# Five elementwise steps of a scan moved from VectorE to GpSimd and ScalarE

## The chip, the cores and the metric

The kernel runs on one core of a Trainium2 chip. A core has five engines that take their instructions in order, each from a queue of its own: TensorE (PE in the profile, its weight loads PEld), VectorE (DVE), ScalarE (ACT), GpSimd (POOL) and SyncE (SP), which only issues DMAs here. They wait for each other by semaphores. Data lies in SBUF and, for the outputs of matmuls, in eight banks of PSUM. The metric is the time of one execution on the device, in microseconds; less is better.

## The reference, cut to what matters

Input are 16 sequences of 512 tokens with 128 channels, float32. A block adds four parts to them, one after the other: an attention with rotated features, a mixture of experts, a selective scan, and the same mixture of experts again; each works on the layer norm of what is there. The change touches the scan, for which the reference is:

```python
xz = jnp.einsum('btd,ed->bte', x, W_in)
xp, z = (xz[..., :D_INNER], xz[..., D_INNER:])          # D_INNER = 256
xc = conv(xp, conv_w) + conv_b                          # causal, 4 taps, by channel
xc = _silu(xc)
ssm = jnp.einsum('bti,si->bts', xc, W_x)
Bp, Cp = (ssm[..., :D_STATE], ssm[..., D_STATE:])       # D_STATE = 16
dt = jax.nn.softplus(jnp.einsum('bti,oi->bto', xc, W_dt) + b_dt)
A = -jnp.exp(A_log)
def step(h, inp):
    x_t, b_t, c_t, dt_t = inp
    dA = jnp.exp(dt_t[..., None] * A)
    h = dA * h + dt_t[..., None] * b_t[:, None, :] * x_t[..., None]
    y_t = jnp.einsum('bds,bs->bd', h, c_t)
    return (h, y_t)
_, ys = lax.scan(step, h0, (tm(xc), tm(Bp), tm(Cp), tm(dt)))
y = (y - mu) * lax.rsqrt(var + LN_EPS) * ln_g + ln_b    # mu, var over the 256 channels
y = y + xc * D_param
y = y * _silu(z)
return jnp.einsum('bti,di->btd', y, W_out)
```

## The kernel before

A sequence is the unit of work: 512 tokens along the free dimension, 128 channels on the partitions (two halves for the 256 channels of the scan). Sequences are taken in pairs. For each of the eight pairs there are four parts: `attention` for both, `ffn` over both together, `scan` for both, `ffn` again with the output.

**The order is made by a planner.** No engine operation is issued where the code describes it. `pe`, `dve`, `act`, `pool` and `g_.add(SP, ...)` put a step into a list, with its engine, an estimated time in microseconds, and the buffers that it reads and writes. `Program.emit` then walks through this list with one clock per engine. Of the steps whose inputs are there and whose buffers are free it takes, for each engine, one that can start within 0.25 us, and among those the one with the smallest `prio`; a step that needs another table of ACT counts as late by 1 us. The engine order that comes of this is fixed in the program, and the real engines follow it whatever the real durations are. `prio` is set in the last lines of `hybrid_block`: the parts of a pair get spans of it (`SPANS`), within which it grows in proportion to the sum of the estimated times. Pair b's scans span b + 1.5 to b + 2.5, the attention of the next pair b + 1 to b + 2, so the two run beside each other. Where the planner sees PE idle for over 0.5 us after little work, it puts in matmuls with zeros (`add_zeros`, L379). A table of ACT is loaded in `emit` (L191) when a step names another one than the last.

**The scan** of one sequence goes through these steps; the lines are those of the profile:

- A layer norm and a transpose (`normed`, L411 to L444). L932 clears the left edge of the tile `pad`.
- For each half c: a projection (L938), its copy to `pad` (ACT, L939), the convolution's first product with its bias (DVE, L942) and three more taps (DVE, L951).
- For each half: a second projection and SiLU for z (L961, L962), SiLU for xc (ACT, L963).
- The matmuls for B and C with their copies (L984, L987), and for the step sizes dt (L996), of which ACT makes |v| (L999) and max(v, 0) (L1000).
- Softplus with a corrected logarithm, for each half o: exp(-|v|) (ACT, L1004), + 1 (DVE, L1005), the logarithm (ACT, L1006), the rounding error of the sum 1 + e (DVE, L1009), the logarithm less this error (DVE, L1013), and added to max(v, 0) (DVE, L1014).
- dt times xc for both halves in one POOL instruction (L1016), and xc times D on ACT (L1020).
- The main part, 32 units of 128 rows (8 channels by 16 states) in 17 steps: PE spreads dt x and dt over the rows (L1050), DVE multiplies by B (L1056), ACT takes exp (L1061), DVE scans along the tokens (L1064), POOL multiplies by C (L1068), PE sums over the states (L1078), and ACT copies y out (L1084).
- The layer norm over the channels: PE's mean (L1096), DVE subtracts it (L1102), ACT squares (L1104), PE's mean of the squares (L1096), and 1/std by `rsqrt`: ACT's logarithm and exponential (L394, L395), then on DVE a Newton step with a square (L397) and three more operations (L398 to L400).
- For each half: y times 1/std (DVE, L1110), times the gain plus xc (DVE, L1113), times z (POOL, L1119). Then the projection (PE, L1126), added to x (DVE, L1129).

`rsqrt` has two callers: here, with a tile of 128x512, and `normed`, with a tile of 128x4.

The tiles `xc`, `z`, `dt`, `sp_u`, `s1`, `Bw` and `Cw` exist once, so one scan follows another. Temporary tiles of 128x512 come from 28 buffers (`half`), with a number for each kind.

**Beside the scan** runs the attention of a later pair. For each pair of units: PE's two products (L541), ACT's logarithm and exponential for a reciprocal (L548, L549), DVE's two operations (L550, with PSUM; L557, with PSUM), POOL's product (L561) and PE's sum (L569). The mixture of experts has a DVE addition (L884) and a GELU (ACT, L887) for each block of rows, the weights by DMA of SP, and a scatter and a gather of rows by DMAs that POOL issues (L797, L909); DVE adds the gathered rows (L921).

Of the kernel before, what the change touches and what calls it, by code (L numbers as in the profile page):

```python
# [12 lines left out]
AF = mybir.ActivationFunctionType  # L13
ALU = mybir.AluOpType
AX = mybir.AxisListType

P = 128
D = 128
N = 512
# [201 lines left out]
def hybrid_block(ctx: ExitStack, tc: tile.TileContext, io: dict, out: bass.AP):  # L221
    nc = tc.nc
# [10 lines left out]
    def sb(tag, shape, bufs=1, dtype=F32):  # L233
        if tag not in places:
            places[tag] = Slots(work, tag, shape, bufs, dtype)
        return Buf(places[tag], tag)
# [22 lines left out]
    def load(name, shape, src=None, eng=None):  # L259
        t = const.tile(list(shape), F32, name=name)  # L260
        (eng or nc.sync).dma_start(out=t, in_=io[name] if src is None else src)
        return t
# [30 lines left out]
    cw = load("cw", [P, NH, KC])  # L293
# [53 lines left out]
    conv_b, b_dt, d_par, ln_g, ln_b = (cols[:, i, :] for i in range(5))  # L347
# [12 lines left out]
    def tmp(kind):  # L360
        return Buf(half, kind)
# [4 lines left out]
    def psum(kind="mm"):  # L366
        return Buf(bank, kind)
# [7 lines left out]
    def pe(us, fn, r, w, claim=(), work=None):  # L375
        g_.add(PE, us, fn, r, w, claim=claim, work=work)
# [6 lines left out]
    def dve(us, fn, r, w):  # L383
        g_.add(DVE, us, fn, r, w)

    def pool(us, fn, r, w):
        g_.add(POOL, us, fn, r, w)

    def act(us, fn, r, w, table=None):
        g_.add(ACT, us, fn, r, w, table)  # L390

    def rsqrt(rs, v, c, shape, tag, us):

        act(us[0], lambda: nc.scalar.activation(rs(), c(v()), AF.Ln, bias=eps), [v], [rs], LNEXP)  # L394
        act(us[0], lambda: nc.scalar.activation(rs(), rs(), AF.Exp, scale=-0.5), [rs], [rs], LNEXP)  # L395
        q = tmp(tag) if shape == [P, N] else sb(tag, shape, 2)
        dve(us[1], lambda: nc.vector.tensor_tensor(q(), rs(), rs(), ALU.mult), [rs], [q])  # L397
        dve(us[1], lambda: nc.vector.scalar_tensor_tensor(q(), c(v()), eps, q(), ALU.add, ALU.mult), [v, q], [q])  # L398
        dve(us[1], lambda: nc.vector.tensor_scalar(q(), q(), -0.5, 1.5, ALU.mult, ALU.add), [q], [q])
        dve(us[1], lambda: nc.vector.tensor_tensor(rs(), rs(), q(), ALU.mult), [rs, q], [rs])  # L400

    def normed(xts, who, bufs):
# [3 lines left out]
        for k, xt in enumerate(xts):  # L406
# [11 lines left out]
            dve(0.6, aggr, [st], [mv])  # L418
            rs = sb("rs", [P, NT], 3)
            rsqrt(rs, mv, lambda t: t[:, :, 1], [P, NT], "q", (0.25, 0.16))  # L420
            mr = sb("mr", [P, NT], 3)
            dve(
# [504 lines left out]
    def scan(b, xs):  # L927
        xt = xs[b]
        _, xnT = normed([xt], "", 2)
        pad, xc, z = sb("s1", [P, NH, KC - 1 + N]), sb("xc", [P, NH, N]), sb("z", [P, NH, N])  # L930
# [5 lines left out]
        for c in range(NH):  # L936
            pz, cv = psum(), tmp("cv")
            pe(MM, lambda c=c, pz=pz: mm(pz(), win[:, c * P : (c + 1) * P], xnT(), start=True, stop=True), [xnT], [pz], [pad, cv, xc, z])  # L938
            act(0.59, lambda c=c, pz=pz: nc.scalar.copy(pad()[:, c, KC - 1 :], pz()), [pz], [(pad, c)])  # L939
            dve(  # L940
                0.55,
                lambda c=c, cv=cv: nc.vector.tensor_scalar(  # L942
                    cv(), pad()[:, c, 0:N], cw[:, c, 0:1], conv_b[:, c : c + 1], ALU.mult, ALU.add
                ),
                [(pad, c), (pad, "edge")],
                [cv],
            )
            for k in range(1, KC):
                dve(
                    0.72,  # L950
                    lambda c=c, k=k, cv=cv: nc.vector.scalar_tensor_tensor(  # L951
                        cv(), pad()[:, c, k : k + N], cw[:, c, k : k + 1], cv(), ALU.mult, ALU.add
                    ),
                    [(pad, c), (pad, "edge"), cv],
                    [cv],
                )
            cvs.append(cv)
            yield
# [31 lines left out]
        dt, ex, up = sb("dt", [P, NH, N]), sb("s1", [P, NH, KC - 1 + N]), sb("sp_u", [P, NH, N])  # L990
# [10 lines left out]
        for o in range(NH):  # L1001
            ln = tmp("sg")
            e_, u_, d_ = (lambda o=o: ex()[:, o, 0:N]), (lambda o=o: up()[:, o, :]), (lambda o=o: dt()[:, o, :])
            act(0.63, lambda e_=e_: nc.scalar.activation(e_(), e_(), AF.Exp, scale=-1.0), [(ex, o)], [(ex, o)], LNEXP)  # L1004
            dve(0.37, lambda e_=e_, u_=u_: nc.vector.tensor_scalar_add(u_(), e_(), 1.0), [(ex, o)], [(up, o)])  # L1005
            act(0.63, lambda u_=u_, ln=ln: nc.scalar.activation(ln(), u_(), AF.Ln), [(up, o)], [ln], LNEXP)  # L1006
            dve(
                0.74,
                lambda e_=e_, u_=u_: nc.vector.scalar_tensor_tensor(u_(), u_(), -1.0, e_(), ALU.add, ALU.subtract),  # L1009
                [(up, o), (ex, o)],  # L1010
                [(up, o)],
            )
            dve(0.7, lambda u_=u_, ln=ln: nc.vector.tensor_tensor(ln(), ln(), u_(), ALU.subtract), [ln, (up, o)], [ln])  # L1013
            dve(0.7, lambda d_=d_, ln=ln: nc.vector.tensor_tensor(d_(), d_(), ln(), ALU.add), [(dt, o), ln], [(dt, o)])  # L1014
        dtx = sb("s1", [P, NH, KC - 1 + N])
        pool(2.35, lambda: nc.gpsimd.tensor_tensor(dtx()[:, :, 0:N], dt(), xc(), ALU.mult), [dt, xc], [dtx])  # L1016

# [5 lines left out]
        y = sb("sp_u", [P, NH, N])  # L1023
# [8 lines left out]
        for n in range(len(two) + 1):  # L1032
            work_ = []
            if n < len(two):
                c, j, q0 = two[n]
# [4 lines left out]
            if n:  # L1040
                c, j, q0 = two[n - 1]
# [15 lines left out]
            if n:  # L1057
                c, j, q0 = two[n - 1]
# [46 lines left out]
        rs = tmp("sg")  # L1105
        var = over_channels(sq, [rs])
        rsqrt(rs, var, lambda t: t, [P, N], "cv", (0.65, 0.68))
        yield
        for c in range(NH):
            dve(0.7, lambda c=c: nc.vector.tensor_tensor(y()[:, c, :], y()[:, c, :], rs(), ALU.mult), [(y, c), rs], [(y, c)])  # L1110
            dve(
                0.74,
                lambda c=c: nc.vector.scalar_tensor_tensor(  # L1113
                    y()[:, c, :], y()[:, c, :], ln_g[:, c : c + 1], xc()[:, c, :], ALU.mult, ALU.add
                ),
                [(y, c), (xc, c)],
                [(y, c)],
            )
            pool(1.27, lambda c=c: nc.gpsimd.tensor_tensor(y()[:, c, :], y()[:, c, :], z()[:, c, :], ALU.mult), [(y, c), (z, c)], [(y, c)])  # L1119
# [19 lines left out]
    def scans(bs):  # L1139
        for b in bs:  # L1140
            yield from scan(b, xs)
# [91 lines left out]
```

## Time and profile before

| | |
|---|---|
| Median of 3 runs | 4292.2 us (4279.41 to 4292.76) |
| Profiled execution | 4297.67 us |
| Its span, first to last instruction | 4295.8 us |
| Instructions | 62640 |
| Mean granted clock of PE | 0.929 |
| DMA | 296.99 MB, mean 69 GB/s |
| Table loads of ACT (L191) | 327 of 1283 ns, 419.5 us |

The profiled execution is one run of its own; sums that are made from the profile are made against its time, and it lies 5.5 us above the median. In a row of the groups of instructions stand the line, the engine, the operation, output and inputs by the program's names, the shapes, the number of instructions, then the busy time in us and the mean of one in ns, and last the idle time of the engine just before them, with what ended most of it. Tiles of `half` are called half, banks of PSUM bank, `pad`, `ex`, `dtx` and the squares s (they share `s1`), and `up` and `y` sp_u.

### The profile page before, as it was taken

Reading aid. Unit: us, or ns where it says so; the run is one execution under the profiler, and the core shown is the slowest. Engines: PE = TensorE matmul, PEld = TensorE weight load, DVE = VectorE, ACT = ScalarE, POOL = GpSimd, SP = SyncE. Lnnn points to the kernel's source line nnn. Section 1 sums busy time; section 2 is a strip of 40 time slices with the busy share of each in tenths; the row PEclk is TensorE's granted clock in tenths of the full one; section 3 lists DMA queues with packets and bytes.
Section 4 is the critical chain, followed back from the end, with each engine's and each line's share of the span. In section 5 each row is a group of like instructions: output and inputs, shape, how many; then the busy total and the mean of one; then the engine's idle time right before and its main releaser. Section 6 shows DMA issues by size and latency. Waiting matters only on the chain. (4 is left out here: it accounts for less than half of the span.)

```text
span 4295.8 us, 62640 instructions
## 1 busy us (share of the span) xinstructions
PE 3967.1 (92%) x20444; PEld 2038.1 (47%) x20444; DVE 3380.3 (79%) x5863; ACT 2850.6 (66%) x4661; POOL 2614.1 (61%) x2202
## 2 busy tenths in 40 slices
PE   7999999989999999999999999999999999987975
PEld 2345344445354454534545345454545445553554
DVE  7975878877888778888797887979788887756772
ACT  6777667567676577766768667686767667544541
POOL 6765855756666466675575765756766656544351
PEclk9999999989999799998999899998999989898996
DMA  2004003104131131310414013131223214141443
GB/s 66 1 27 127 9 26 87 48 28 120 33 95 56 28 114 54 104 36 28 125 45 124 12 47 109 56 115 32 71 72 93 67 30 121 44 126 38 115 127 107
DMA packets 397770, 296.99 MB, mean 69 GB/s; under 512 B 29290, under 2 KB 340596, under 8 KB 397444
## 3 DMA queue, kind: packets, MB, share of 16 engines
q1 hardware_dynamic: 380324, 258.87, 21.0%
q0 software_dynamic: 16544, 33.66, 2.7%
q8 instruction: 163, 2.67, 0.3%
q14 instruction: 163, 1.34, 0.1%
q10 hardware_dynamic: 576, 0.46, 0.0%
HBM read 244.32 MB, written 48.56 MB: 68 GB/s over the span
## 5 line engine op out<-in xcount | busy, mean ns | idle before, releaser
L561 POOL TENSOR_TENSOR half<-half,half 128x512 f32<-128x512 f32 x1024 | 1293.6, 1284 | 556.8 <-DVE half L557 438.9
L1068 POOL TENSOR_TENSOR half<-half,Cw 128x512 f32<-128x512 f32 x512 | 641.9, 1272 | 544.8 <-DVE half L1064 464.5
L550 DVE TENSOR_TENSOR half<-bank,half 128x512 f32<-128x512 f32 x1024 | 689.3, 683 | 190.3 <-ACT half L549 172.7
L541 PE MATMUL bank<-rot,krot 32*128 32x512 f32 x2048 | 770.5, 672 | 29.3 <-DVE half L550 15.9
L557 DVE SCALAR_TENSOR_TENSOR half<-half,bank 128x512 f32<-128x512 f32 x1024 | 667.3, 679 | 162.2 <-PE bank L541 151.5
L548 ACT ACTIVATE half<-bank 128x512 f32<-128x512 f32 x1024 | 598.8, 585 | 281.9 <-PE bank L541 275.1
L549 ACT ACTIVATE half<-half 128x512 f32<-128x512 f32 x1024 | 645.1, 630 | 30.9
L1064 DVE TENSOR_TENSOR_SCAN half<-bank,half 128x512 f32<-128x512 f32 x512 | 599.5, 1207 | 74.8 <-ACT bank L1061 73.3
L541 PE MATMUL bank<-raw,kraw 32*128 32x512 f32 x2048 | 616.3, 664 | 10.7 <-DVE half L550 5.9
L1061 ACT ACTIVATE bank<-bank,A 128x512 f32<-128x512 f32 x512 | 319.2, 658 | 254.7 <-PE bank L1050 249.6
L379 PE MATMUL bank<-cos,zero 128*128 128x512 f32 x850 | 479.0, 672 | 0.0
L879 PE MATMUL bank<-half,w 128*128 128x128 f32 x3000 | 401.1, 283 | 47.1 <-DMA w<-in_W 32.7
L879 PEld LDWEIGHTS bank<-half,w 128*128 128x128 f32 x3000 | 362.8, 194 | 157.8 <-DVE half L884 44.3
L191 ACT ACT_TABLE_LOAD x327 | 419.5, 1283 | 5.7
L1056 DVE TENSOR_TENSOR half<-bank,Bw 128x512 f32<-128x512 f32 x512 | 328.8, 682 | 104.7 <-PE bank L1050 104.3
L891 PEld LDWEIGHTS bank<-w,half 128*128 128x128 f32 x3000 | 353.2, 193 | 100.6 <-ACT half L887 68.5
L891 PE MATMUL bank<-w,half 128*128 128x128 f32 x3000 | 379.3, 281 | 18.9 <-ACT half L887 18.2
L1050 PE MATMUL bank<-dt,over 32*128 32x512 f32 x1024 | 373.6, 672 | 16.7 <-DVE half L550 16.6
L569 PE MATMUL bank<-half,v_sp 128*32 128x512 f32 x2048 | 356.7, 625 | 14.5 <-POOL half L561 13.9
L541 PEld LDWEIGHTS bank<-raw,kraw 32*128 32x128 f32 x2048 | 176.3, 192 | 337.4 <-DVE half L550 69.5
L541 PEld LDWEIGHTS bank<-rot,krot 32*128 32x128 f32 x2048 | 242.4, 192 | 164.7 <-DVE half L550 60.1
L1050 PE MATMUL bank<-s,over 32*128 32x512 f32 x1024 | 307.2, 667 | 8.3 <-POOL s L1016 4.5
(248 smaller groups left out, 5387.1 us busy)
## 6 DMA issues: line engine op xcount, KB each, us to landing
w<-in_W SPq DMA_DIRECT2D x750, 256.0 KB
half<-inr SPq DMA_DIRECT2D x43, 256.0 KB
outr<-half SPq DMA_DIRECT2D x43, 256.0 KB
half<-ins SPq DMA_DIRECT2D x38, 256.0 KB
outs<-half SPq DMA_DIRECT2D x38, 256.0 KB
x<-in_x SPq DMA_DIRECT2D x16, 256.0 KB
out<-x SPq DMA_DIRECT2D x16, 256.0 KB
inr<-xn,sir POOLq DMA_INDIRECT x136
```

The costliest lines, as they stand in the source:

```text
L379: mm(to, zero, cos, start=False, stop=False)
L541: mm(to(), km()[rows, j * P : (j + 1) * P], q()[rows, :], start=True, stop=True)
L548: act(0.62, lambda r0=r0, den=den: nc.scalar.activation(r0(), den(), AF.Ln), [den], [r0], LNEXP)
L549: act(0.62, lambda r0=r0: nc.scalar.activation(r0(), r0(), AF.Exp, scale=-1.0), [r0], [r0], LNEXP)
L550: dve(0.67, lambda w=w, r0=r0, den=den: nc.vector.tensor_tensor(w(), den(), r0(), ALU.mult), [den, r0], [w])
L557: lambda w=w, num=num: nc.vector.scalar_tensor_tensor(w(), w(), -2.0, num(), ALU.add, ALU.mult),
L561: pool(1.27, lambda w=w, r0=r0: nc.gpsimd.tensor_tensor(w(), w(), r0(), ALU.mult), [w, r0], [w])
L879: mm(ph()[:, at], w1()[:, at], xbT()[:, i * P : (i + 1) * P], start=True, stop=True)
L891: mm(py()[:, i * P : (i + 1) * P], quad(h)[:, c, :], w2()[:, c, :], start=(c == 0), stop=(c == NF - 1))
L1050: mm(to(), over[rows, j, :], v()[rows, c, 0:N], start=True, stop=True)
L1064: lambda pd=pd, db=db: nc.vector.tensor_tensor_scan(db(), pd(), db(), 0.0, ALU.mult, ALU.add),
L1068: pool(1.3, lambda db=db: nc.gpsimd.tensor_tensor(db(), db(), Cw(), ALU.mult), [db, Cw], [db])
```

## The change

Five operations go to other engines; what they compute stays, and so do all tiles. L397 becomes a Square on ACT where the tile is 128x512. L942 becomes an Identity on ACT, with scale and bias by partition. L1013, L1014 and L1110 become the same operation on POOL. The planner's estimates change with the engine, 0.55 to 0.63, 0.68 to 0.65 and 0.7 to 1.27 us, so the order of all steps from the first scan on is made anew.

```diff
@@ rsqrt
-        dve(us[1], lambda: nc.vector.tensor_tensor(q(), rs(), rs(), ALU.mult), [rs], [q])
+        if shape == [P, N]:
+            act(us[0], lambda: nc.scalar.activation(q(), rs(), AF.Square), [rs], [q])
+        else:
+            dve(us[1], lambda: nc.vector.tensor_tensor(q(), rs(), rs(), ALU.mult), [rs], [q])
@@ scan
-            dve(
-                0.55,
-                lambda c=c, cv=cv: nc.vector.tensor_scalar(
-                    cv(), pad()[:, c, 0:N], cw[:, c, 0:1], conv_b[:, c : c + 1], ALU.mult, ALU.add
+            act(
+                0.63,
+                lambda c=c, cv=cv: nc.scalar.activation(
+                    cv(), pad()[:, c, 0:N], AF.Identity, scale=cw[:, c, 0:1], bias=conv_b[:, c : c + 1]
                 ),
...
-            dve(0.7, lambda u_=u_, ln=ln: nc.vector.tensor_tensor(ln(), ln(), u_(), ALU.subtract), [ln, (up, o)], [ln])
-            dve(0.7, lambda d_=d_, ln=ln: nc.vector.tensor_tensor(d_(), d_(), ln(), ALU.add), [(dt, o), ln], [(dt, o)])
+            pool(1.27, lambda u_=u_, ln=ln: nc.gpsimd.tensor_tensor(ln(), ln(), u_(), ALU.subtract), [ln, (up, o)], [ln])
+            pool(1.27, lambda d_=d_, ln=ln: nc.gpsimd.tensor_tensor(d_(), d_(), ln(), ALU.add), [(dt, o), ln], [(dt, o)])
...
-            dve(0.7, lambda c=c: nc.vector.tensor_tensor(y()[:, c, :], y()[:, c, :], rs(), ALU.mult), [(y, c), rs], [(y, c)])
+            pool(1.27, lambda c=c: nc.gpsimd.tensor_tensor(y()[:, c, :], y()[:, c, :], rs(), ALU.mult), [(y, c), rs], [(y, c)])
```

## The prediction

> **What bounds the kernel now.** I read the busy shares first, then the windows (busy time per stretch, with and without the padding matmuls), then the groups of instructions, then the timeline of one stretch.
>
> ```profile
> PE 3967.1 (92%) x20444; PEld 2038.1 (47%) x20444; DVE 3380.3 (79%) x5863; ACT 2850.6 (66%) x4661; POOL 2614.1 (61%) x2202
> L379 PE MATMUL bank<-cos,zero 128*128 128x512 f32 x850 | 479.0, 672 | 0.0
> ```
>
> PE's 92% overstates it: 479.0 us are the planner's matmuls with zeros (L379), issued where it foresaw an idle PE. Without them PE has 3488 us of work, DVE 3380. These two lead; ACT and POOL have a third of the span free.
>
> By line, the memset L932 that opens a scan and the sum L1129 that closes one stand next to each other: from 558 to 4192 us one scan follows another. Each has a **main part** (L1056 to L1068) and, between two main parts, an **edge**: the end of one scan (L1102 to L1129) and the start of the next (L932 to L1016). All moved instructions lie in the edges. Two edges and one main part, all engines (columns: length, then busy us and instructions of PE, PEld, DVE, ACT, POOL; clock; DMA):
>
> ```profile
> 3178.00:3253.00 75.00, 72.51 (x332) 36.52 (x332) 67.52 (x162) 49.82 (x82) 47.79 (x43) 0.91 0.19 55
> 2417.00:2514.00 97.00, 91.12 (x366) 45.47 (x366) 81.88 (x189) 59.83 (x108) 56.53 (x48) 0.84 0.11 33
> 3253.00:3426.00 173.00, 165.78 (x928) 86.14 (x926) 139.79 (x193) 124.25 (x201) 118.02 (x99) 0.96 0.29 83
> ```
>
> And the zeros (PE and PEld alone) in the two edges:
>
> ```profile
> 3178.00:3253.00 75.00, 1.12 (x2) 0.30 (x2) 0.91 0.19 55
> 2417.00:2514.00 97.00, 12.46 (x20) 4.55 (x20) 0.84 0.11 33
> ```
>
> The reader is to see two kinds of edge. In the first DVE (90%) and PE (97%, nearly no zeros) are both full. In the second DVE has 84%, PE 81% without its zeros: DVE and the order of the work lead. POOL is at 58 to 64% in both. The second kind is at 1908, 2417, 2925 and 3426 us (10 to 12.6 us of zeros each); the eight other edges up to 3253 have 0.8 to 6 us. The three edges after 3673 us have no attention beside them, and DVE is at 50 to 70%.
>
> **The change, part by part.** What DVE loses:
>
> ```profile
> L1009 DVE SCALAR_TENSOR_TENSOR sp_u<-sp_u,s 128x512 f32<-128x512 f32 x32 | 36.8, 1148 | 4.8 <-ACT half L1006 4.6 <-issue 0.2
> L1013 DVE TENSOR_TENSOR half<-half,sp_u 128x512 f32<-128x512 f32 x32 | 31.4, 981 | 1.1
> L1014 DVE TENSOR_TENSOR dt<-dt,half 128x512 f32<-128x512 f32 x32 | 24.4, 761 | 1.0
> L1110 DVE TENSOR_TENSOR sp_u<-sp_u,half 128x512 f32<-128x512 f32 x32 | 22.7, 709 | 0.5
> L397 DVE TENSOR_TENSOR half<-half 128x512 f32<-128x512 f32 x16 | 18.8, 1178 | 4.6 <-ACT half L395 4.0 <-issue 0.6
> L942 DVE TENSOR_SCALAR half<-s,cw,cols 128x512 f32<-128x512 f32 x32 | 17.7, 554 | 10.8 <-ACT s L939 8.5 <-POOL s L932 1.9 <-ACT rs L395 0.3
> ```
>
> L1013, L1014, L1110, L397 and L942: 31.4 + 24.4 + 22.7 + 18.8 + 17.7 = 115.0 us, or **7.2 us a scan**. At their medians (693, 692, 691, 691, 542 ns) it would be 94.8 us; the other 20 us are long single cases (L1013 up to 3.28 us).
>
> What is added. POOL gets 96 products and sums of 128x512. The same operation takes 1272 ns there (L1068): 122 us, 7.6 a scan. ACT gets 32 Identities with a scale and a bias per partition, at 804 ns by L1020, and 16 Squares at 630 ns by L549: 25.7 + 10.1 = 35.8 us, 2.2 a scan. ACT's 2.2 lie beside other work (it is at 62% over the edges). What would uncover them is a table load more; Square (L1104) and Identity (L1020) run now without one of their own, so I count none. No DMA is moved. On POOL's queue the issues of the gathers and scatters (L909, L797, about 1.0 us each) now share the edge with six more instructions; POOL goes from 48 to about 55 us in an edge of 75, which still fits.
>
> **A cost that before cannot show: what six more POOL instructions do to the rest of DVE.** L1009 and L1113, DVE operations with both inputs in SBUF, have medians of 686 and 752 ns but means of 1148 and 1099; L550, with an input in PSUM, has 683 mean and at most 693. So some operations on SBUF alone are held, 0.46 and 0.35 us on the mean, which I put down to POOL working beside them. Bounds for the price: nothing (the moved operations leave DVE, and so can no longer collide), or a whole POOL instruction each, 6 x 1.27 = 7.6 us a scan. I take the mean of the two rows, 0.40 x 6 = 2.4 us a scan, as they are the nearest; net relief **7.2 - 2.4 = 4.8 us a scan**.
>
> The Trainium skill (Perfetto Trace Analysis, Optimizing Scalar/DVE Operations) speaks against this change: DVE and GpSimd share an SBUF read port, so that moving work between these two may not help. SBUF — State Buffer (Who interferes with whom) makes it a lock: whoever comes second waits for the whole other instruction. Held strictly, by that rule the sum would keep only ACT's part (18.8 + 17.7 = 36.5 us, 2.3 a scan), which by the sum below would be 4 x 2.3 + 8 x 1.15 - 10 = 8 us less, 4284 us; the rows of L1009 and L1113 show such holds, but by 0.4 us and not by 1.27.
>
> **Length of the chain.** The scan's own chain becomes longer. One start, DVE and then POOL:
>
> ```profile
> 3239.28 0.69 DVE L1013 TENSOR_TENSOR half<-half,sp_u 128x512 f32<-128x512 f32 x1
> 3240.01 0.69 DVE L1014 TENSOR_TENSOR dt<-dt,half 128x512 f32<-128x512 f32 x1
> ...
> 3241.94 1.01 POOL L797 DMA_INDIRECT inr<-xn,sir  x1 [3.25 <-DVE sp_u L1009]
> ...
> 3242.98 1.29 POOL L561 TENSOR_TENSOR half<-half,half 128x512 f32<-128x512 f32 x1
> ...
> 3244.22 2.35 POOL L1016 TENSOR_TENSOR s<-dt,xc 128x1024 f32<-128x1024 f32 x1
> ```
>
> From L1013's start to the end of the second L1014 DVE needs 3.5 us; four POOL instructions in a row need 5.1: +1.6. In the shown case POOL stood idle 3.25 us just there, and L1016 then waited for POOL's own queue, so most of the 1.6 is covered; where the queue is full it is not. At the scan's end L397 becomes shorter (1.18 to 0.63: -0.55), and two L1110 and two L1119 on POOL make 5.4 us where the mixed chain takes 5.0 (0.71 + 1.10 + 0.71 + 1.10 + 1.42): +0.4. The convolution: 0.80 for 0.55, +0.25, the second half beside the first. Together +1.7, up to +3.0 with one attention product queued in between (1.27). I take **+2.5**, nearer to the upper end as each handing-over to POOL adds a queue. Queued behind a POOL instruction that waits are attention's L561 and the gathers; for L561 wait PE's L569 and then buffers of attention.
>
> **The sum.** Edges with zeros: DVE leads, the whole relief counts: 4 x 4.8 = 19. The eight other edges with attention beside them: PE is as full as DVE, so I count half: 8 x 2.4 = 19. The first start and the three late edges: DVE isn't full, only the chain's length counts: 4 x 2.5 = +10. In all -28 us. The profiled execution took 4297.67 us (span 4295.8); minus 28 is 4270. The median of the three runs shown is 5.5 us lower, 4292.2: minus 28 gives **4264 us**. What is late next: PE in the first kind of edge, ACT's and PE's hand-overs to DVE (L550 waits 172.7 us for L549, L557 151.5 for PE) in the main part, which nothing here shortens.
>
> **Rivals.**
> - *Full relief.* Nothing collides, and the freed DVE time counts in all twelve edges: 12 x 7.2 = 86, less 10: 4216 us. For it: DVE waits little in the edges (7.5 us of 75). Against it: PE has 97% in the first kind.
> - *No effect.* The planner recomputes the whole order from its own costs; PE is full, or the freed time fills with zeros (L379): about 4290 us. For it: main parts make up 2336 of the 3556 us, and their DVE share (80%) isn't touched.
> - *Slower: POOL's queue takes the place of DVE's.* POOL works strictly in order, and the chain hands over to it twice a scan. If three attention products or gathers (1.27 each) stand ahead of its instructions, the chain grows by 1.7 + 3.8 = 5.5 us, x 16 = 88 us, less the 38 of relief: 4342 us. It decides from the point where the chain grows by more than the 2.4 to 4.8 us of relief, in the edges where scan and attention both wait. For it: L1016 waited 75.1 us for L1014, so POOL already stands still behind this chain. Against it: POOL's 58 to 64%.
> - *Another order.* The list of steps is laid out anew, and table loads (327 x 1283 ns) or zeros may come out otherwise: twenty loads are 26 us on ACT, either way. I count this as spread around each case, not as a case.
>
> **Chances.** The forecast (4264, by itself 4225 to 4279) 0.42; full relief 0.12; no effect 0.16; slower 0.30. Faster by over 0.3% (about what a measurement of this kernel can tell from no change): 0.54; within 0.3%: 0.16; slower: 0.30. The range reaches from a little beyond full relief to the slower rival's time: 4205 to 4345.
>
> **What would show it.** Right: DVE near 3290 us busy, POOL near 2735, ACT near 2885; edges of the second kind about 5 us shorter, main parts unchanged; L1009, L1113 or L951 longer on the mean by some 0.1 to 0.4 us. Wrong: POOL's wait ahead of the two sums or of L1016 grows beyond 75 us; attention's L569 waits longer for L561 (137.5 us now); edges as long as before with more zeros; a number of table loads other than 327.

## The result, and the profile after

The changed kernel takes 4344.5 us (median of 4 runs, 4338.58 to 4354.63), against 4288.0 for the kernel before in 4 runs: ratio **1.0136 [1.011, 1.0163]**, slower by some 57 us. The profiled execution took 4345.52 us (span 4343.4). In the changed kernel every line from the old L397 on is 3 higher: the old L397 to L400 are L400 to L403, L561 is L564, L1013 is L1016, L1016 is L1019, and so on; the Square on ACT is L398.

Its page, busy times, then zeros and table loads:

```profile
PE 4001.5 (92%) x20468; PEld 2058.8 (47%) x20468; DVE 3345.5 (77%) x5719; ACT 2858.0 (66%) x4692; POOL 2727.7 (63%) x2298
...
L379 PE MATMUL bank<-cos,zero 128*128 128x512 f32 x874 | 487.6, 666 | 0.0
...
L191 ACT ACT_TABLE_LOAD x310 | 397.7, 1283 | 5.5
```

144 instructions that took DVE 115.0 us are gone, but DVE's busy time fell by 34.9 us only (3380.3 to 3345.5). So the instructions that stayed took about 80 us more of DVE, **5.0 us a scan**. POOL is where it was expected. The table loads are 17 fewer, so they are not the cause.

The edge that stood at 3178 to 3253 us before, and the one of the second kind (columns as in the prediction):

```profile
3198.00:3288.00 90.00, 83.41 (x367) 44.42 (x370) 77.29 (x160) 56.41 (x94) 62.91 (x55) 0.87 0.17 49
2417.00:2514.00 97.00, 91.22 (x365) 44.62 (x358) 76.94 (x178) 62.78 (x110) 58.75 (x50) 0.84 0.10 31
```

The first is 90 us where it was 75. It has some more work in it (367 matmuls for 332), but also a clock of 0.87 where it had 0.91, and DVE is busy for 77 us with 160 instructions, where it was for 67.5 with 162. The second kind is as long as before: from scan to scan 98 us (2413 to 2511) where it was 97. Read off the scans (L1064), the first twelve edges went from 992 to 1035 us in all and the main parts that follow them from 1979 to 1951; the first main part grew from 91 to 112 and the three late edges from 227 to 241.

Which DVE rows became longer? Groups by shape, of before and then of after:

```profile
L397 DVE TENSOR_TENSOR q<-rs 128x4 f32<-128x4 f32 x64 | 35.0, 551 | 10.1 <-ACT rs L395 10.1
L400 DVE TENSOR_TENSOR rs<-rs,q 128x4 f32<-128x4 f32 x64 | 27.2, 428 | 1.0
```

```profile
L400 DVE TENSOR_TENSOR q<-rs 128x4 f32<-128x4 f32 x64 | 47.5, 746 | 5.7 <-ACT rs L395 5.5
...
L403 DVE TENSOR_TENSOR rs<-rs,q 128x4 f32<-128x4 f32 x64 | 39.5, 618 | 1.5
L1116 DVE SCALAR_TENSOR_TENSOR sp_u<-sp_u,cols,xc 128x512 f32<-128x512 f32 x32 | 38.9, 1227 | 3.0 <-POOL sp_u L1113 3.0
...
L1012 DVE SCALAR_TENSOR_TENSOR sp_u<-sp_u,s 128x512 f32<-128x512 f32 x32 | 25.8, 827 | 5.3 <-ACT half L1009 5.0
```

The first two work on 4 columns, in the layer norms that open the parts (`rsqrt` by `normed`), which the change doesn't touch. Their median is 0.16 us and their longest case 3.2 us; 10 and 7 of the 64 took over 1 us in before, 16 and 13 in after. The two operations between them grew too: L401 from 417 to 550 ns, and L402, which has one input only, from 328 to 408. L1116 went from 1099 to 1227; L1012, the other row on which the price was formed, became shorter (1148 to 827).

One such case, near the end of the edge at 3198 to 3288. First the timeline of DVE, then of POOL, then of PE (start, length, line, number of instructions joined, idle time before):

```profile
3266.00 1.27 DVE L560 SCALAR_TENSOR_TENSOR half<-half,bank 128x512 f32<-128x512 f32 x2
3267.19 0.68 DVE L553 TENSOR_TENSOR half<-bank,half 128x512 f32<-128x512 f32 x1
3267.79 2.44 DVE L924 SCALAR_TENSOR_TENSOR x<-y,wts,x 128x128 f32<-128x128 f32 x2
3270.15 0.68 DVE L553 TENSOR_TENSOR half<-bank,half 128x512 f32<-128x512 f32 x1
3270.75 2.89 DVE L400 TENSOR_TENSOR q<-rs 128x4 f32<-128x4 f32 x1
...
3273.94 0.17 DVE L402 TENSOR_SCALAR q<-q 128x4 f32<-128x4 f32 x1
3274.14 3.20 DVE L403 TENSOR_TENSOR rs<-rs,q 128x4 f32<-128x4 f32 x1
```

```profile
3267.45 1.29 POOL L1016 TENSOR_TENSOR half<-half,sp_u 128x512 f32<-128x512 f32 x1
3268.82 1.26 POOL L1017 TENSOR_TENSOR dt<-dt,half 128x512 f32<-128x512 f32 x1
3270.24 1.00 POOL L800 DMA_INDIRECT inr<-xn,sir  x1 [0.15 <-issue]
3271.26 2.35 POOL L1019 TENSOR_TENSOR s<-dt,xc 128x1024 f32<-128x1024 f32 x1
3273.78 1.01 POOL L800 DMA_INDIRECT inr<-xn,sir  x1 [0.17 <-DVE q L400]
3274.82 2.49 POOL L564 TENSOR_TENSOR half<-half,half 128x512 f32<-128x512 f32 x2
```

```profile
3270.88 1.12 PE L544 MATMUL bank<-rot,krot 32*128 32x512 f32 x2 [1.79 <-DVE half L553]
...
3275.91 1.16 PE L839 MATMUL bank<-sW,hs 128*128 128x128 f32 x8
3278.29 1.39 PE L1053 MATMUL bank<-s,over 32*128 32x512 f32 x4 [1.22 <-DVE half L560]
...
3279.96 2.08 PE L839 MATMUL bank<-sW,hs 128*128 128x128 f32 x8
```

Lay the first two over each other. L924 (128x128) ends 0.15 us after L1017, L400 (3273.64) with L1019 (3273.61), and L403 (3277.34) with the second of two L564 in a row (3277.31): the small DVE operations end when POOL's reading does. Of these POOL instructions only L1016 and L1017 are new. They hold L924; L400 comes later by it and meets L1019, and L403 meets L564, both of which the kernel before has too. So at this place a new instruction costs by itself, and also by moving other operations into the way of old ones. L553, which takes one input from PSUM, runs at its usual 0.68 us beside L1016. PE then waits twice for DVE, for 1.79 and 1.22 us, and eight matmuls of L839 that took 1.16 us take 2.08 after the second wait: the granted clock there is 0.50.

The waits of after, for the rival with POOL's queue (us, times, longest):

```profile
POOL half L564 <- DVE half L560: 371.1, 166, 9.3
PEld bank L572 <- POOL half L564: 132.7, 178, 9.0
POOL half L1016 <- DVE sp_u L1012: 75.5, 14, 22.1
...
ACT xc L1023 <- POOL s L1019: 6.3, 3, 4.6
...
PEld bank L1053 <- POOL s L1019: 4.0, 3, 1.6
```

L572 waits 132.7 us for POOL (137.5 before), and the end of the chain through POOL, L1019, keeps ACT and PE waiting for some 13 us only (2.8 of PE are not in the fence). In this order POOL's queue isn't what is late.

### The profile page after: what moved, and what is told of

Same layout as the page of the kernel before. It is cut to its first block, busy times and chain, and to the rows that moved or that the text cites. A ratio compares the mean times of both kernels' runs of the same rounds, so it can differ in the third digit from the quotient of the medians.

```text
span 4343.4 us, 62747 instructions
## 1 busy us (share of the span) xinstructions
PE 4001.5 (92%) x20468; PEld 2058.8 (47%) x20468; DVE 3345.5 (77%) x5719; ACT 2858.0 (66%) x4692; POOL 2727.7 (63%) x2298
## 5 line engine op out<-in xcount | busy, mean ns | idle before, releaser
L564 POOL TENSOR_TENSOR half<-half,half 128x512 f32<-128x512 f32 x1024 | 1288.7, 1281 | 433.5 <-DVE half L560 371.1
L553 DVE TENSOR_TENSOR half<-bank,half 128x512 f32<-128x512 f32 x1024 | 689.1, 682 | 207.0 <-ACT half L552 202.8
L560 DVE SCALAR_TENSOR_TENSOR half<-half,bank 128x512 f32<-128x512 f32 x1024 | 665.0, 677 | 145.2 <-PE bank L544 134.4
L1064 ACT ACTIVATE bank<-bank,A 128x512 f32<-128x512 f32 x512 | 318.9, 658 | 282.3 <-PE bank L1053 277.9
L572 PE MATMUL bank<-half,v_sp 128*32 128x512 f32 x2048 | 359.6, 626 | 13.8 <-POOL half L564 13.6
```

The lines of the kernel that those rows point to most:

```text
L553: dve(0.67, lambda w=w, r0=r0, den=den: nc.vector.tensor_tensor(w(), den(), r0(), ALU.mult), [den, r0], [w])
L560: lambda w=w, num=num: nc.vector.scalar_tensor_tensor(w(), w(), -2.0, num(), ALU.add, ALU.mult),
L564: pool(1.27, lambda w=w, r0=r0: nc.gpsimd.tensor_tensor(w(), w(), r0(), ALU.mult), [w, r0], [w])
```

## The experiments

Theories. **Holding**: POOL's new instructions, as they read SBUF, stop DVE's operations with two inputs from SBUF. **Chain**: the scan's chain through POOL's queue is longer. **Order**: the planner's new order is worse by itself, whatever the engines do. All ratios are to runs of the kernel before in the same batch. `dve(...)`, `pool(...)` and `act(...)` tell the planner on which engine and for how long a step runs; the call inside says which engine does it. So an order can be kept while the work goes elsewhere.

**Order and engines apart.** e1 keeps the order of before and issues the five operations on POOL and ACT:

```diff
-            dve(0.7, lambda u_=u_, ln=ln: nc.vector.tensor_tensor(ln(), ln(), u_(), ALU.subtract), [ln, (up, o)], [ln])
+            dve(0.7, lambda u_=u_, ln=ln: nc.gpsimd.tensor_tensor(ln(), ln(), u_(), ALU.subtract), [ln, (up, o)], [ln])
...
```

> The planner is told the old engines and times (0.55, 0.68, 0.7 us on DVE), so the order of all steps is that of the kernel before, while the five operations are issued on POOL and ACT as in the changed kernel. Theory ORDER (the loss of 1.36% comes from the newly made order of the steps): 4275 to 4305 us, like before. Theory QUEUE (the longer chain through POOL's queue costs the time): 4330 to 4370, as slow as the change or slower, since the order makes no room for it. Theory PORT (POOL's instructions hold DVE's operations on SBUF): 4325 to 4350, with DVE's busy time near 3345 us as in the changed kernel; where the holding is the same but the time is not, PORT falls.

e2 has the order of after, with all five issued on DVE:

```diff
-            pool(1.27, lambda u_=u_, ln=ln: nc.gpsimd.tensor_tensor(ln(), ln(), u_(), ALU.subtract), [ln, (up, o)], [ln])
+            pool(1.27, lambda u_=u_, ln=ln: nc.vector.tensor_tensor(ln(), ln(), u_(), ALU.subtract), [ln, (up, o)], [ln])
...
```

> The converse: the planner is told the new engines and times (0.63 and 0.65 us on ACT, 1.27 us on POOL), so the order is that of the changed kernel, but all five operations are issued on DVE as in the kernel before. ORDER: 4330 to 4355 us, as slow as the change. QUEUE: 4270 to 4300, as the longer chain is gone and DVE only gets its 115 us back. PORT: 4275 to 4300, DVE's busy time near 3380 us.

e1: 4380.1 us, **1.0218 [1.0191, 1.0246]**. e2: 4368.1, 1.0176 [1.0137, 1.0215]. e1 is slower than either kernel. e2 is slower than before and no faster than after, which no theory had foretold: crossing order and engines doesn't split the loss into two parts. e1 does show the chain. Who waits for dt times xc, in before and then in e1:

```profile
POOL s L1016 <- DVE dt L1014: 75.1, 10, 30.5
...
ACT xc L1020 <- POOL s L1016: 26.8, 10, 4.7
...
PEld bank L1050 <- POOL s L1016: 10.5, 8, 2.0
```

```profile
ACT xc L1023 <- POOL s L1019: 69.5, 16, 6.9
...
PEld bank L1053 <- POOL s L1019: 42.7, 15, 6.0
PE bank L1053 <- POOL s L1019: 29.9, 13, 3.7
```

In e1 PE and ACT wait at nearly every scan's start for POOL: 142 us where before has 42 (37.3 and 4.5 of PE that is not in the fence). From the end of the second L1009 to the start of the product with xc it is 2.3 us in before, 6.0 in e1, 5.3 in after (means of the twelve edges).

DVE is held far less in e1 than in after, by the same new instructions:

```profile
PE 3990.8 (91%) x20444; PEld 2047.3 (47%) x20444; DVE 3294.4 (75%) x5719; ACT 2879.5 (66%) x4709; POOL 2730.2 (62%) x2298
```

115.0 us less work shows as 85.9 us less busy time (3380.3 to 3294.4), so the rest of DVE takes 29 us more, 1.8 a scan, where after has 5.0. What six POOL instructions cost DVE thus depends on the order.

**Parts of the change, planned anew.** e3 moves only the two sums, e4 only ACT's two operations; the other lines stay as in before.

```diff
-            dve(0.7, lambda u_=u_, ln=ln: nc.vector.tensor_tensor(ln(), ln(), u_(), ALU.subtract), [ln, (up, o)], [ln])
+            pool(1.27, lambda u_=u_, ln=ln: nc.gpsimd.tensor_tensor(ln(), ln(), u_(), ALU.subtract), [ln, (up, o)], [ln])
...
```

> Only the two sums of the step sizes go to POOL (64 of the 96 POOL instructions), with the order made anew for it. QUEUE: most of the loss, 4320 to 4345 us, and the edges that are full on PE and DVE are again about 12 us longer than before. PORT: two thirds of the loss, near 4325. ORDER: another order again, anywhere from 4260 to 4350.

> Only the convolution's first product and the square go to ACT, with the order made anew. QUEUE and PORT: no POOL instruction is added and DVE loses 36 us, so 4270 to 4295 us, no slower than before. ORDER: anywhere from 4260 to 4350; slower than 4305 would speak for it.

e3: 4303.3, 1.0033 [1.0017, 1.005]. e4: 4313.0, 1.0061 [1.0037, 1.0085], though nothing in it uses POOL more. Each has an order of its own, and what that is worth by itself the next experiments measure.

**Parts of the change in the order of before.** f1, f2 and f3 are e1 with only the two sums, only the product with 1/std, and only ACT's two.

```diff
-            dve(0.7, lambda c=c: nc.vector.tensor_tensor(y()[:, c, :], y()[:, c, :], rs(), ALU.mult), [(y, c), rs], [(y, c)])
+            dve(0.7, lambda c=c: nc.gpsimd.tensor_tensor(y()[:, c, :], y()[:, c, :], rs(), ALU.mult), [(y, c), rs], [(y, c)])
```

> The order of the kernel before is kept (the planner is told DVE and 0.7 us), and only the two sums of the step sizes are issued on POOL. With all five moved in this order the time was 4380 us against 4284. QUEUE: the sums carry most of it, since the stretch from the second L1009 to L1016 grew there from 2.3 to 6.0 us a scan: 16 x 3.7 = 59 us, so 4325 to 4355. PORT: 64 of 96 POOL instructions, so two thirds of 96, also near 4348, and DVE would be held longer in the sum over its other rows by 20 us or more. If ORDER were the only cause, 4275 to 4305.

> The order of the kernel before is kept, and only the product with 1/std is issued on POOL. QUEUE: the scan's end (L1102 to the end of L1119) grew by 1.9 us a scan with all five moved: 16 x 1.9 = 30 us, so 4300 to 4325. PORT: a third of 96, near 4316. ORDER alone: 4275 to 4300.

> The order of the kernel before is kept, and only the convolution's first product and the square are issued on ACT. DVE loses 36 us, ACT gets 36 us, no POOL instruction is added. QUEUE and PORT: 4270 to 4295, no loss. If a bare mismatch between order and engines costs time whatever is moved: 4300 to 4330.

f1: 4332.7, 1.0075 [1.0037, 1.0113]. f2: 4349.8, 1.0131 [1.0096, 1.0166]. f3: 4298.7, 1.0013 [0.9995, 1.003]. Together 2.2%, as e1. The product with 1/std costs more than either theory gave it (4300 to 4325). f3 is the cleanest test of the relief: the order of before, POOL untouched, and

```profile
PE 3965.7 (92%) x20444; PEld 2037.3 (47%) x20444; DVE 3346.9 (78%) x5815; ACT 2880.6 (67%) x4709; POOL 2613.2 (61%) x2202
```

DVE has 33.4 us less to do than in before (3380.3), nearly as much as it lost in after, and no time is won that could be told from none.

**What an order is worth.** The four estimates of the moved steps are changed by 0.02 or 0.04 us, far less than an instruction's length; the work and its engines stay. n2 is before with 0.02 less, n1 with 0.02 more, n7 with 0.04 less; n3 and n4 are after with 0.02 more and less.

```diff
-                0.55,
+                0.53,
...
-            dve(0.7, lambda u_=u_, ln=ln: nc.vector.tensor_tensor(ln(), ln(), u_(), ALU.subtract), [ln, (up, o)], [ln])
+            dve(0.68, lambda u_=u_, ln=ln: nc.vector.tensor_tensor(ln(), ln(), u_(), ALU.subtract), [ln, (up, o)], [ln])
...
```

> No instruction changes its engine: only the planner's estimates of four of the moved steps are 0.02 us higher (0.57 and 0.72 us), so that the order is made anew for the same work. If the order of the kernel before is one among equals: 4270 to 4300 us. If it is a lucky or a picked one, as ORDER needs, the new order costs by itself: 4300 to 4345.

> As the run with the estimates 0.02 us higher, now 0.02 us lower (0.53 and 0.68 us on DVE): the same work on the same engines in another order. With the order of before a picked one: 4300 to 4345 again; if the run before it was an unlucky draw: 4270 to 4300.

> The kernel before with the estimates of four steps 0.04 us lower (0.51 and 0.66 us), another draw of its order. If the change costs by itself, the draws without it stay lower on the middle: 4235 to 4310. If only the draw counts: 4235 to 4345.

> The changed kernel with the planner's estimates of four of its five moved steps 0.02 us higher (0.65 and 1.29 us): its work and engines in another order. If orders of the changed kernel scatter like those of the kernel before, between 4310 and 4370 us; if the change costs by itself and orders add a little, 4335 to 4355. Below 4300 would say that the 1.36% was the draw of the order alone.

> The changed kernel with the planner's estimates of four moved steps 0.02 us lower (0.61 and 1.25 us), another draw of its order. The draws so far: 4344 and 4324 with the change, 4289, 4328 and 4235 without. If the change costs by itself: 4310 to 4360. If only the draw counts: anywhere from 4235 to 4345, below 4300 as likely as above.

| Work of before | ratio | Work of after | ratio |
|---|---|---|---|
| as it is | 1 | as it is | 1.0136 [1.011, 1.0163] |
| n1 | 1.007 [1.0048, 1.0091] | n3 | 1.0091 [1.0063, 1.0119] |
| n2 | **0.9891 [0.9859, 0.9922]** | n4 | 1.0085 [1.0064, 1.0107] |
| n7 | 0.9991 [0.9973, 1.0008] | | |

The same work in another order differs by 1.8% (n2 to n1), more than the change itself. The means are 0.9988 and 1.0104: by them about 1.2% of the loss belongs to the work's new engines and the rest to this draw, an estimate from four and three draws only. All three orders of after have a higher ratio than all four of before. n2, 4234.9 us, is faster than both kernels by its order alone. e3 and e4 lie within the scatter of orders, so no verdict on their parts rests on them.

**Two probes of DVE and POOL in the order of before.** x1 puts six products that nothing reads behind the second L1014; b1 issues two products of POOL (L1016, L1119) on DVE instead.

```diff
-            dve(0.7, lambda d_=d_, ln=ln: nc.vector.tensor_tensor(d_(), d_(), ln(), ALU.add), [(dt, o), ln], [(dt, o)])
+            def last(o=o, d_=d_, ln=ln):
+                nc.vector.tensor_tensor(d_(), d_(), ln(), ALU.add)
+                for _ in range(6 if o == NH - 1 else 0):
+                    nc.vector.tensor_tensor(ln(), d_(), d_(), ALU.mult)
+
+            dve(0.7, last, [(dt, o), ln], [(dt, o)])
```

> The order and the engines of the kernel before, with six DVE products of 128x512 more in each scan, whose result nobody reads, issued behind the scan's last sum L1014: DVE is busy 6 x 0.69 = 4.2 us longer in each edge, 66 us in all, and no step of the scan's chain waits for it. The prediction counted 4.8 us of DVE in an edge in full or by half, which by the same reckoning (four edges in full, eight by half, none in the rest) makes 4.2 us worth 4 x 4.2 + 8 x 2.1 = 34 us: 4318 to 4335. QUEUE (only the chain's length counts, DVE's load in the edge does not): 4284 to 4305.

```diff
-        pool(2.35, lambda: nc.gpsimd.tensor_tensor(dtx()[:, :, 0:N], dt(), xc(), ALU.mult), [dt, xc], [dtx])
+        pool(2.35, lambda: nc.vector.tensor_tensor(dtx()[:, :, 0:N], dt(), xc(), ALU.mult), [dt, xc], [dtx])
...
```

> The opposite move in the order of the kernel before: the POOL products of the scan's start (L1016, 2.35 us) and of its end (L1119, 1.42 us) are issued on DVE, the planner still told POOL. DVE gets about 16 x 1.2 + 32 x 0.7 = 42 us more, the chain gets shorter by 2.35 - 1.2 and by about 0.7 us at its end, and two hand-overs to POOL go. QUEUE: faster by 16 x 1.9 = 30 us or more, 4235 to 4265. If DVE's load counts as predicted: 2.6 us an edge dearer, 4300 to 4320. If any mismatch of order and engines costs: 4310 to 4350.

x1: 4388.2, 1.0232 [1.0199, 1.0266]: 100 us for products that took DVE 101 us, 1.05 us each. It isn't a clean test, since the extra products also stand ahead of the scan's own start (from the start of L1016 to the first scan 11.5 us became 18.3, means of the twelve edges). What it shows is that DVE time at this place, ahead of the scan's start, counts in full. b1: 4301.0, 1.0029 [1.0011, 1.0047]; I had expected it faster. DVE's busy time rose by 14.6 us (3380.3 to 3394.9) though it got 45.3 us more to do (22.8 + 22.5), so some 31 us of holding went, and again no time was won. Why it is even a little slower stays open.

**POOL as busy, but without reading.** q1 and q2 put three fills of 128x400, which only write, in the place of each of the 96 new POOL instructions, in the order of after and of before. They lose two waits with the operands, so q3 and q4 do it better: the same operation on one column, which keeps every wait, and three fills of 350 columns.

```diff
+    def touch(t, other, op, v):
+        nc.gpsimd.tensor_tensor(t[:, 0:1], t[:, 0:1], other[:, 0:1], op)
+        for _ in range(3):
+            nc.gpsimd.memset(t[:, 1:351], v)
...
-            pool(1.27, lambda u_=u_, ln=ln: nc.gpsimd.tensor_tensor(ln(), ln(), u_(), ALU.subtract), [ln, (up, o)], [ln])
+            pool(1.27, lambda u_=u_, ln=ln: touch(ln(), u_(), ALU.subtract, 0.0), [ln, (up, o)], [ln])
...
```

> The changed kernel with its order; each of the 96 new POOL instructions is replaced by three fills of 128x400 with a constant, which read nothing (about 1.3 us together by the fill of v_sp, 1901 ns for 2176 columns). It leaves out both sums and the product with 1/std, so dt and y are constants. PORT (what costs is that POOL's reads hold DVE's operations on SBUF): DVE's operations lose some 20 to 30 us of waiting and the time falls to 4300 to 4325. QUEUE (POOL's place in the chain costs): 4335 to 4355, as the change.

> The order of the kernel before with the engines of the change, the 96 POOL instructions again replaced by three fills of 128x400 (both sums and the product with 1/std are left out). With the real instructions 4380 us. PORT: 4300 to 4340. QUEUE: 4365 to 4390, the stretch from the second L1009 to L1016 still near 6 us.

> The order of the change; each of the 96 new POOL instructions becomes the same operation on one column, which waits for all that the real one waits for, and three fills of 128x350 (about 1.2 us in all). It leaves out both sums and the product with 1/std on the other columns. PORT: as fast as with the fills alone, 4290 to 4320 us, DVE near 3295 us busy. QUEUE: 4330 to 4355.

> The same replacement in the order of the kernel before with the engines of the change (4380 us with the real instructions, 4374 with the fills alone); it leaves out the same parts. QUEUE: 4360 to 4390, as nothing in the chain changed. PORT: below 4340.

In the order of after: q1 4303.8, 1.0015 [0.9994, 1.0036]; **q3 4290.1, 0.9998 [0.998, 1.0016]**. In the order of before: q2 4373.8, 1.0159 [1.0133, 1.0185]; q4 4364.8, 1.0171 [1.0135, 1.0207]. q3's page, the same edge, and the two rows on 4 columns:

```profile
PE 3946.7 (92%) x20468; PEld 2028.4 (47%) x20468; DVE 3278.9 (76%) x5719; ACT 2857.8 (67%) x4692; POOL 2732.0 (64%) x2586
```

```profile
3153.00:3232.00 79.00, 75.05 (x366) 38.80 (x368) 68.38 (x159) 55.89 (x93) 61.72 (x71) 0.96 0.18 55
```

```profile
L400 DVE TENSOR_TENSOR q<-rs 128x4 f32<-128x4 f32 x64 | 36.6, 575 | 6.7 <-ACT rs L395 6.4
...
L403 DVE TENSOR_TENSOR rs<-rs,q 128x4 f32<-128x4 f32 x64 | 26.8, 419 | 1.5
```

The same order, the same number of instructions on PE, DVE and ACT, and POOL as busy as in after: yet the edge is 79 us, its clock 0.96, and PE is busy for 55 us less with the same 20468 matmuls, which goes with its clock (0.938 over the span against 0.926). Of the 66.6 us that DVE has less than in after, 29.4 are L400, L401 and L403 (4 columns) and 17.3 the two forms of L924 (128 columns). The place shown above, in q3 (L929 is L924, L565 is L560):

```profile
3216.88 1.27 DVE L565 SCALAR_TENSOR_TENSOR half<-half,bank 128x512 f32<-128x512 f32 x2
...
3218.67 0.73 DVE L929 SCALAR_TENSOR_TENSOR x<-y,wts,x 128x128 f32<-128x128 f32 x2
...
3219.92 0.15 DVE L400 TENSOR_TENSOR q<-rs 128x4 f32<-128x4 f32 x1
...
3220.36 0.41 DVE L402 TENSOR_SCALAR q<-q 128x4 f32<-128x4 f32 x1
3220.81 0.16 DVE L403 TENSOR_TENSOR rs<-rs,q 128x4 f32<-128x4 f32 x1
```

```profile
3219.00 1.27 POOL L453 MEMSET half<- 128x350 f32 x3
...
3220.36 1.28 POOL L453 MEMSET dt<- 128x350 f32 x3
```

2.44, 2.89 and 3.20 us have become 0.73, 0.15 and 0.16 beside POOL's fills; L400 and L403 now run before the product with xc starts (L1024 there, 3223.05), and don't meet it. From the second L1009 to that product it is 5.7 us, no less than in after, so the longer chain through POOL is still there and costs nothing. So in the order of after the whole loss goes when the new instructions no longer read.

In the order of before the fills change little: DVE falls from 3294.4 to 3284.7 us and the ratio from 1.0218 to 1.0171, with intervals that overlap. The 1.7% that stay there go with the waits for POOL at the scan's start, which are 178 us in q4 (142 in e1); that they are the whole cause wasn't tested by itself. The fills put constants in the place of data; q4 has the same constants and is only 0.5% faster than e1, the missing reads included, so the constants don't explain the 1.4% between after and q3.

## Why the prediction was wrong

**The first step that failed** is the price of holding: "I take the mean of the two rows, 0.40 x 6 = 2.4 us a scan, as they are the nearest". Measured are 5.0 us a scan by DVE's busy time, (115.0 - 34.9) / 16, so 2.2 us of relief are left of the 4.8; 4.2 of the 5.0 go in q3 (66.6 / 16). The upper bound, 7.6 a scan, held. But the price isn't a constant (e1 pays 1.8, less than the prediction took), and the size alone doesn't turn the sign: with 2.2 us of relief the prediction's own sum is 4 x 2.2 + 8 x 1.1 - 10 = 8 us less. What the sum has no term for is what a hold delays beyond DVE: it charges holds as DVE time against the relief, while between after and q3 the same order loses 1.4% by them, PE's waits and its lower clock included.

The rows of L1009 and L1113 were the wrong ones to average: their own operation is 0.7 us long, and six new instructions of POOL were taken to cost what these rows lose on the mean. Those that paid most were the rows of 4 and 128 columns (29.4 and 17.3 of the 66.6 us between after and q3), which lose up to 20 times their length; before had them already (551 and 428 ns on the mean on 4 columns, for a median of 0.16 us), and I didn't look at them, as the change doesn't name them.

The Trainium skill's rule (SBUF — State Buffer, Who interferes with whom) was nearer: an operation with two inputs from SBUF that comes second waits for the whole POOL instruction that reads, and a POOL instruction that only writes doesn't stop it. The timelines of after and q3 agree in both: 2.89 and 3.20 us against 0.15 and 0.16; but L403 waited for two instructions, and had started before either. The forecast by that rule, 4284 us, was wrong nevertheless, as it had no price for what the holds delay.

**A second step failed with it**: that relief of DVE counts, "in full" in the second kind of edge and "half" in the others. f3 gives 33.4 us of relief in a fixed order and wins nothing; q3 has 101 us less of DVE than before (3380.3 to 3278.9) and takes the same time, though its order is another draw and its chain is longer. A busy share of 84 to 90% didn't show that DVE leads. What sets the pace instead isn't shown; that it is the fixed order with its hand-overs to ACT and PE is a guess. Without the reads the change was worth nothing in its own order.

**The rivals.** "POOL's queue takes the place of DVE's" has the right sign, and its 4342 us is within 3 us of the median, but in the order that the planner made it was not the mechanism: L1019 kept others waiting for some 13 us, where before had 42. So the nearness of the number is luck. A loss of that kind is what e1 and q4 show, where the order isn't made anew. "Full relief" fell with f3 and q3. "No effect" was right on the relief and missed the holds.

**Another order** was priced at 26 us either way. The scatter measured is -54 to +36 us around the median of before's runs (n2: 4234.9 against 4288.6; n1: 4327.7 against 4292.1), so any forecast of one comparison of this kernel has that much luck in it, whatever its mechanism.

**What held**: POOL at 2727.7 us (2735 foretold), ACT's Identity at 814 ns and Square at 630 (804 and 630 foretold), and 1.28 to 1.32 us for each new POOL instruction (1.27 foretold). The chain at the scan's start did become longer, by 3.0 us where 1.6 were foretold. What didn't hold: DVE was to be near 3290 us busy (the prediction's own 4.8 us a scan give 3303) and was at 3345.5; L1009 was to become longer and became shorter; edges of the second kind were to become 5 us shorter, and the one shown stayed at 97.

**Open.** How much of the 57 us is PE's lower clock and how much the holds themselves: the time with the granted clock at half was 609 us in before, 647 in after and 534 in q3, which can't be the whole of it, as before and q3 take the same time, and it was not varied by itself. Why the same new instructions hold DVE for 29 us in one order and 80 in another: the place shown suggests that it is a matter of which operations they push together, but that was not followed over the whole kernel. Whether e3's and e4's parts gain or lose beyond the luck of their orders.

## What to carry to other kernels

Before moving work from DVE to POOL, list DVE's operations on SBUF by shape, the tiny ones first, and compare median, mean and longest case: here a wide gap was holding, and new POOL instructions that read added to it, by 29 us of DVE in one order and 80 in another. So measure it in the order that will run. A busy share near 90% is not a proof that an engine leads; take some work off it without adding any elsewhere, in an order that stays fixed, and see whether the time moves. With a list scheduler, measure a few orders of the same work before believing a difference of 1%.

## What was unexpected of the hardware

A 128x4 operation of 0.16 us was held for up to 3.2 us, and behind two POOL instructions in a row, not only one (L403 ended 0.03 us after the second L564); it had started 0.68 us before the first of them, while POOL was busy with a gather's issue (L800). Gaps of 1.2 to 1.8 us on PE were followed by matmuls at half the clock (eight L839: 1.16, then 2.08 us); that the gaps are the cause was not tested. And POOL fills of 128x350 (0.39 us each) beside the same DVE work left L400, L403 and L924 at their medians, but not L402, which has one input: it took 0.41 us beside a fill, where its median is 0.17.
